# A selective-scan kernel: the copy of y moves to the end of its slot, and one more product with C moves to GpSimd

## The chip, the cores and the metric

The kernel runs on one core of a Trainium2 chip, in one launch. The metric is the device time in microseconds (us); the time before is the median of 3 runs. A core has TensorE (PE in the profile), VectorE (DVE), ScalarE (ACT), GpSimd (POOL) and SyncE (SP), whose queue issues the DMA transfers. All data are 32-bit floats.

## The reference

The input x has shape 2 x 256 x 256 x 128 (images, rows, columns, channels). Two layers follow each other, each on a group-normalised x and added to x: an attention along one image axis, and a selective state-space scan. Only the second one is touched by the change. Cut to what matters:

```python
xi, z = jnp.split(x @ in_proj_w.T, 2, axis=-1)        # 256 channels each
xs = silu(depthwise_conv3x3(xi) + conv_b)             # as (channel, position)
dts, Bs, Cs = split(x_proj_w @ xs)                    # 8, 16 and 16 rows
delta = softplus(dt_w @ dts + dt_b)
A = -exp(A_logs)                                      # 256 channels x 16 states
# for every position, channel d and state n:
h = exp(delta * A) * h + (delta * xs) * B
y[d] = sum_n(h[d, n] * C[n]) + Ds[d] * xs[d]
y = layernorm(y) * silu(z)
out = x + y @ out_proj_w.T
```

## The kernel before

An attention stage comes first, in the first 2500 us or so. The rest of the time is the scan layer.

**How the scan is tiled.** One step takes 4 rows of an image, T = 1024 positions. There are 64 steps to an image and 128 in all. A step is cut into NU = 32 units. A unit is one tile of 128 partitions x 1024 positions: 32 channels times 4 states on the partitions. Unit number t in its step is h (two halves of 128 channels, 16 units each), m (four groups of 4 states) and q (four groups of 32 channels), with q running fastest. So the units go through in one long order, 4096 of them, and a step is called a round below. In a round, unit 11 is h=0, m=2, q=3; it is the last one that reads the C rows of its (h, m).

**What a unit needs.**

- `drive` (line 966): hb = delta * xs * B, on GpSimd, for two units at a time (a pair, 2048 elements in the free axis). `hb` has 3 buffers of a pair.
- `decay` (line 956): da = exp(delta * A), on ScalarE, into PSUM. There are two of these tiles, `da0` and `da1`, for even and odd units.
- `scan` (line 978): the recurrence, on VectorE. It writes h over `da` (PSUM), or over `hb` (SBUF) if the unit is "pooled".
- the product yc = h * C, with C repeated over the partitions in the tile `cc`: on VectorE for each single unit (`product`, line 992), or on GpSimd for the pair if it is pooled (`products`, line 1001). GpSimd's product takes h from `hb`, in SBUF; that is why a pooled unit leaves h there. `yc` has 4 buffers of a pair, `cc` and `bb` have 2.
- `remember` (line 983): a copy of the last column of h, on ScalarE, the start of the same unit in the next step.
- `add_up` (line 1024): TensorE adds the rows of yc over states into the PSUM tile `y`, four units at a time. `start_up` (line 1015) begins `y` with Ds * xs.
- `y_out` (line 1037): ScalarE copies the finished `y` to SBUF, twice in a round. The next `start_up` needs `y` free.

Five pairs are pooled in each round: the pairs that begin at units 6, 14, 22, 26 and 30. The other 22 units have their product on VectorE.

**What sets the order.** The loop at the end of the function writes the order of the four compute engines by hand: in slot t it emits, among others, the decay of unit t+1, the scan and product of unit t, then the pieces of work of other stages that are planned for this slot (`others` on any engine, then `on_pe`), then `start_up` and `add_up` for earlier units, and last `remember` of unit t. Each engine takes its own instructions in that order. The order on SyncE's queue is left to the framework's scheduler.

The other pieces prepare the next step (`project`: convolution `u_ps`, gate `z_ps`, sizes `dt_ps` and their copies on ScalarE `xs`, `sz`, `delta`) and finish the last one (`finish_row`: `yt`, norm `yn`, `yd`, product with the gate `yg` on VectorE line 871, `o_ps`, copy `ob`). Those that matter here are, in slot 19: two `yn` passes (line 852) and a copy `sz` (line 713); in slot 20: SiLU of z, which is a table load, one pass of 2048 elements and another table load (lines 718 and 619); in slot 12: softplus in the same form (line 763); in slot 28: SiLU of xs (line 695). `y_out` falls into slots 3 and 19.

Of the kernel before, what the change touches and what calls it, by code (L numbers as in the profile page):

```python
# [10 lines left out]
ALU = mybir.AluOpType  # L11
# [10 lines left out]
def attn_then_ssm_kernel(  # L22
# [26 lines left out]
    nc = tc.nc  # L49
# [78 lines left out]
    NSG = NS // SR  # L128
# [149 lines left out]
    with ExitStack() as actx:  # L278
# [242 lines left out]
        end = B * NA  # L521
# [65 lines left out]
    NU = NCG * NSG  # L587
    NM = NQ * NSG

    POOLED = (6, 14, 22, 26, 30)  # L590
    s1 = ctx.enter_context(tc.tile_pool(name="s1", bufs=1))
    s2 = ctx.enter_context(tc.tile_pool(name="s2", bufs=2))
    s3 = ctx.enter_context(tc.tile_pool(name="s3", bufs=3))
# [318 lines left out]
    def unit(t):  # L912

        k, i = divmod(t, NU)
        h, i = divmod(i, NM)
        m, q = divmod(i, NQ)
        return k, h, m, q

    spreads, repeats = {}, {}

    def fetch(t):
        k, h, m, q = unit(t)
        v = given[k]
        if q == 0:

            for name, row in (("bb", m * SR), ("cc", NS + m * SR)):
                tl = repeats[name, k, h, m] = s2.tile([P, T], F32, name=name)
                nc.sync.dma_start(
                    out=tl, in_=v["bc"][row : row + SR, :].partition_broadcast(CQ)
                )  # L930
        if m == 0:

            for name in ("delta", "du"):
                if name == "delta":
                    tl = s5.tile([P, T], F32, name="delta_r")
                elif q % 2 == 0:
                    pair = spreads["pair", k, h, q] = s3.tile([P, 2, T], F32, name="du_r")
                    tl = pair[:, 0, :]
                else:
                    tl = spreads["pair", k, h, q - 1][:, 1, :]  # L940
                spreads[name, k, h, q] = tl
                nc.sync.dma_start(
                    out=tl,
                    in_=v[name][h, q * CQ : (q + 1) * CQ, :]
                    .unsqueeze(1)
                    .to_broadcast([CQ, SR, T]),
                )

    def pooled(t):
        return t % NU - t % 2 in POOLED  # L950

    def decay(t):
        k, h, m, q = unit(t)
        da = units[t]["da"] = ps_d.tile([P, T], F32, name=f"da{t % 2}")
        g = h * NQ + q
        nc.scalar.activation(  # L956
            da, spreads["delta", k, h, q], AF.Exp, scale=a_neg[:, g, m : m + 1]
        )

    def drive(t):  # L960

        k, h, m, q = unit(t)
        hb = s3.tile([P, 2, T], F32, name="hb")
        units[t] = {"pair": hb, "hb": hb[:, 0, :]}
        units[t + 1] = {"hb": hb[:, 1, :]}
        nc.gpsimd.tensor_tensor(  # L966
            hb,
            spreads["pair", k, h, q],
            repeats["bb", k, h, m].unsqueeze(1).to_broadcast([P, 2, T]),
            ALU.mult,  # L970
        )

    def scan(t):
        k, h, m, q = unit(t)
        u = units[t]
        st = states_of[steps[k][0]][:, h * NQ + q, m : m + 1]
        u["h"] = u["hb"] if pooled(t) else u["da"]
        nc.vector.tensor_tensor_scan(u["h"], u["da"], u["hb"], st, ALU.mult, ALU.add)  # L978

    def remember(t):  # L980
        k, h, m, q = unit(t)
        st = states_of[steps[k][0]][:, h * NQ + q, m : m + 1]
        nc.scalar.copy(st, units[t]["h"][:, T - 1 : T])  # L983

    def product(t):
        k, h, m, q = unit(t)
        u = units[t]
        if t % 2 == 0:
            yc = s4.tile([P, 2, T], F32, name="yc")
            for i in range(2):  # L990
                units[t + i]["yc"] = yc[:, i, :]
        nc.vector.tensor_tensor(u["yc"], u["h"], repeats["cc", k, h, m], ALU.mult)  # L992

    def products(t):

        k, h, m, q = unit(t)
        hb = units[t]["pair"]
        yc = s4.tile([P, 2, T], F32, name="yc")
        for i in range(2):
            units[t + i]["yc"] = yc[:, i, :]  # L1000
        nc.gpsimd.tensor_tensor(  # L1001
            yc, hb, repeats["cc", k, h, m].unsqueeze(1).to_broadcast([P, 2, T]), ALU.mult
        )
# [3 lines left out]
    def start_up(t):  # L1007

        k, h, _, _ = unit(t)
        xr = s1.tile([P, T], F32, name="xr")  # L1010
        nc.sync.dma_start(out=xr, in_=given[k]["xs"][h])
        y = outs["y"] = ps_y.tile([P, T], F32, name="y")
        for i in range(NB):
            cols = slice(i * TB, (i + 1) * TB)
            nc.tensor.matmul(y[:, cols], d_diag[:, h, :], xr[:, cols], start=True, stop=False)

    def add_up(t):

        _, _, m, _ = unit(t)
        y = outs["y"]  # L1020
        for i in range(NB):
            cols = slice(i * TB, (i + 1) * TB)
            for q in range(NQ):
                nc.tensor.matmul(  # L1024
                    y[q * CQ : (q + 1) * CQ, cols],
                    sel,
                    units[t + q]["yc"][:, cols],
                    start=False,
                    stop=(m == NSG - 1),
                )  # L1030
        for q in range(NQ):
            del units[t + q]

    def y_out(t):
        k, h, _, _ = unit(t)
        ys[k, h] = s2.tile([P, T], F32, name=f"ys{h}")
        nc.scalar.copy(ys[k, h], outs["y"])
# [4 lines left out]
    end = len(steps) * NU  # L1042
# [7 lines left out]
    with tc.manual_schedule(engines=engines):  # L1050
        for t in range(min(slots), max(slots) + 1):
            if 0 <= t + AHEAD < end:
                fetch(t + AHEAD)
            if 0 <= t < end and t % (NU * NSTEP) == 0:
                st = s1.tile([P, NCG, NSG], F32, name="state")
                nc.gpsimd.memset(st, 0.0)
                states_of[steps[t // NU][0]] = st
            if 0 <= t + 3 < end and t % 2:
                drive(t + 3)
            if 0 <= t - 2 < end and t % 2 == 0 and pooled(t - 2):  # L1060
                products(t - 2)
            if 0 <= t + 1 < end:
                decay(t + 1)
            if 0 <= t < end:
                scan(t)
                if not pooled(t):
                    product(t)
            if 0 <= t - 7 < end and unit(t - 7)[2:] == (NSG - 1, 0):
                y_out(t - 7)
            others, on_pe = slots.pop(t, ((), ()))  # L1070
            for piece, args in others:
                piece(*args)
            for piece, args in on_pe:
                piece(*args)
            if 0 <= t - 5 < end and (t - 5) % NM == 0:
                start_up(t - 5)
            if 0 <= t - 6 < end and (t - 6) % NQ == 0:
                add_up(t - 6)
            if 0 <= t < end:
                remember(t)  # L1080


# [35 lines left out]
```

## Time and profile before

| what | value |
|---|---|
| time, median of 3 | 16278.99 us (16275.81 to 16286.14) |
| span of the profiled run | 16298.5 us |
| VectorE busy | 14642.8 us, 90% |
| TensorE busy | 13879.5 us, 85% |
| GpSimd busy | 13035.7 us, 80% |
| ScalarE busy | 10842.9 us, 67% |
| one round of 106.00 us in the middle of the scan layer (7973.40 to 8079.40): VectorE / GpSimd / TensorE / ScalarE busy | 102.30 / 99.56 / 89.75 / 73.63 us |

The shares of the whole span mix two layers. The round is the unit to think in: 128 of them follow each other, and a microsecond that leaves the chain of each round is 128 us of the whole. Busy time says which engine has no room; what an engine waited for, and what waits behind it in its own order, says what a change of order can give.

### The profile page before, as it was taken

Reading aid. Unit: us, or ns where it says so; the run is one execution under the profiler, and the core shown is the slowest. Engines: PE = TensorE matmul, PEld = TensorE weight load, DVE = VectorE, ACT = ScalarE, POOL = GpSimd, SP = SyncE. Lnnn points to the kernel's source line nnn. Section 1 sums busy time; section 2 is a strip of 40 time slices with the busy share of each in tenths; the row PEclk is TensorE's granted clock in tenths of the full one; section 3 lists DMA queues with packets and bytes.
Section 4 is the critical chain, followed back from the end, with each engine's and each line's share of the span. In section 5 each row is a group of like instructions: output and inputs, shape, how many; then the busy total and the mean of one; then the engine's idle time right before and its main releaser. Section 6 shows DMA issues by size and latency. Waiting matters only on the chain. (4 is left out here: it accounts for less than half of the span.)

```text
span 16298.5 us, 178168 instructions
## 1 busy us (share of the span) xinstructions
PE 13879.5 (85%) x59451; PEld 7046.9 (43%) x59451; DVE 14642.8 (90%) x12484; ACT 10842.9 (67%) x20003; POOL 13035.7 (80%) x3216
## 2 busy tenths in 40 slices
PE   6999997888888888888888888888888888888886
PEld 5877783333333333333333333333333333333333
DVE  7665555999999999999999999999999999999998
ACT  3555554667666666766666666666776676677665
POOL 0111114999999999999999999999999999999998
PEclk9999998999999999999999999999999999999998
DMA  4322223666666666666666666666666666666665
GB/s 183 132 92 78 94 78 135 236 233 237 237 230 233 237 233 236 239 232 235 232 237 232 232 229 234 236 234 234 238 234 233 234 237 233 236 239 232 234 232 180
DMA packets 1428907, 3452.13 MB, mean 212 GB/s; under 512 B 119784, under 2 KB 711184, under 8 KB 1407504
## 3 DMA queue, kind: packets, MB, share of 16 engines
q1 hardware_dynamic: 1427984, 3440.73, 61.0%
q8 instruction: 468, 7.67, 0.2%
q14 instruction: 455, 3.73, 0.1%
HBM read 2752.41 MB, written 687.88 MB: 211 GB/s over the span
## 5 line engine op out<-in xcount | busy, mean ns | idle before, releaser
L966 POOL TENSOR_TENSOR hb<-du_r,bb 128x2048 f32<-128x2048 f32 x2048 | 9237.6, 4538 | 354.3 <-DVE da L978 296.2
L978 DVE TENSOR_TENSOR_SCAN da<-da,state,hb 128x1024 f32<-128x1024 f32 x2816 | 6607.2, 2346 | 163.1 <-ACT da L956 160.2
L676 PE MATMUL u_ps<-xn,w_tap 128*128 128x512 f32 x9216 | 4481.8, 629 | 617.0 <-ACT state L983 607.5
L956 ACT ACTIVATE da<-delta_r,a_neg 128x1024 f32<-128x1024 f32 x4096 | 4588.5, 1120 | 91.8 <-ACT state L983 0.4
L992 DVE TENSOR_TENSOR yc<-da,cc 128x1024 f32<-128x1024 f32 x2816 | 3449.1, 1225 | 287.3 <-PE y L1024 113.8
L1001 POOL TENSOR_TENSOR yc<-hb,cc 128x2048 f32<-128x2048 f32 x640 | 2908.7, 4545 | 527.6 <-ACT state L983 493.0
L978 DVE TENSOR_TENSOR_SCAN hb<-da,state,hb 128x1024 f32<-128x1024 f32 x1280 | 2941.9, 2336 | 199.1 <-ACT state L983 166.4
L676 PEld LDWEIGHTS u_ps<-xn,w_tap 128*128 128x128 f32 x9216 | 1762.1, 201 | 3108.4 <-issue 2110.6
L1024 PE MATMUL y<-yc,sel 128*32 128x512 f32 x16384 | 2409.3, 712 | 16.6 <-POOL yc L1001 16.6
L435 POOL TENSOR_TENSOR x1g<-xc,bo_all 128x512 f32<-128x512 f32 x256 | 315.7, 1271 | 1844.3 <-DVE stats L484 1843.1
L983 ACT COPY state<-da 128x1 f32<-128x1 f32 x2816 | 458.2, 163 | 1266.7 <-DVE yc L992 1262.4
L828 PE MATMUL yt<-centre,ys 128*128 128x256 f32 x4096 | 1029.7, 395 | 250.2 <-ACT ob L889 250.2
L1024 PEld LDWEIGHTS y<-yc,sel 128*32 128x32 f32 x16384 | 477.4, 121 | 1743.3 <-issue 1518.6
L702 PE MATMUL z_ps<-xn,w_z 128*128 128x512 f32 x1024 | 691.8, 763 | 628.2 <-ACT sz L713 389.6
L385 ACT ACTIVATE e<-s_ps,nmx 128x256 f32<-128x256 f32 x1024 | 479.4, 478 | 967.9 <-DVE nmx L376 956.7
L983 ACT COPY state<-hb 128x1 f32<-128x1 f32 x1280 | 247.0, 193 | 1262.2 <-DVE hb L978 1262.2
L828 PEld LDWEIGHTS yt<-centre,ys 128*128 128x128 f32 x4096 | 741.3, 191 | 430.1 <-ACT ob L889 347.8
L744 PE MATMUL dt_ps<-xd,w_dt 8*128 8x512 f32 x1024 | 611.7, 678 | 345.2 <-ACT state L983 193.7
L889 ACT COPY ob<-o_ps 128x256 f32<-128x256 f32 x512 | 191.0, 373 | 948.6 <-PE o_ps L879 948.0
L879 PE MATMUL o_ps<-w_out,szr 128*128 128x128 f32 x4096 | 799.2, 277 | 0.0
L879 PE MATMUL o_ps<-w_out,yg 128*128 128x128 f32 x4096 | 797.9, 277 | 0.0
L352 DVE TENSOR_TENSOR v<-v_ps,bv_all 128x512 f32<-128x512 f32 x256 | 177.1, 692 | 594.5 <-PE v_ps L345 594.5
(133 smaller groups left out, 17404.3 us busy)
## 6 DMA issues: line engine op xcount, KB each, us to landing
bb<-bc_d SPq DMA_DIRECT2D x1024, 512.0 KB, 4.2
cc<-bc_d SPq DMA_DIRECT2D x1024, 512.0 KB, 4.8
delta_r<-delta_d SPq DMA_DIRECT2D x1024, 512.0 KB, 6.6
du_r<-du_d SPq DMA_DIRECT2D x1024, 512.0 KB, 5.5
sz_d<-sz SPq DMA_DIRECT2D x128, 1024.0 KB, 6.6
szr<-sz_d SPq DMA_DIRECT2D x512, 256.0 KB, 4.1
xs_d<-xs SPq DMA_DIRECT2D x128, 1024.0 KB, 9.0
xr<-xs_d SPq DMA_DIRECT2D x256, 512.0 KB, 5.7
```

What stands on the lines that cost most here:

```text
L676: nc.tensor.matmul(o["u"], w_tap[:, h, tap, :], xn[:, i * RB + dy : i * RB + dy + RB, dx : dx + W], start=(tap == 0), stop=(tap == 8),)
L702: nc.tensor.matmul(o["z"], w_z[:, h, :], xn[:, 1 + i * RB : 1 + (i + 1) * RB, 1 : W + 1], start=True, stop=True,)
L744: nc.tensor.matmul(o["dt"], w_dt[:, h, :], o["xd"][0:DR, i * TB : (i + 1) * TB], start=True, stop=True,)
L828: nc.tensor.matmul(o["yt"][:, j, :], ys[k, h][:, t0 + j * P : t0 + (j + 1) * P], centre[:, (1 - h) * P : (1 - h) * P + DI], start=(h == 0) ...
L879: nc.tensor.matmul(o["o"][:, j, :], o[by][:, h, j * P : (j + 1) * P], w_out[:, i, h, :], start=False, stop=(j == WT - 1 and h == NH - 1 an ...
L956: nc.scalar.activation(da, spreads["delta", k, h, q], AF.Exp, scale=a_neg[:, g, m : m + 1])
L966: nc.gpsimd.tensor_tensor(hb, spreads["pair", k, h, q], repeats["bb", k, h, m].unsqueeze(1).to_broadcast([P, 2, T]), ALU.mult,)
L978: nc.vector.tensor_tensor_scan(u["h"], u["da"], u["hb"], st, ALU.mult, ALU.add)
L983: nc.scalar.copy(st, units[t]["h"][:, T - 1 : T])
L992: nc.vector.tensor_tensor(u["yc"], u["h"], repeats["cc", k, h, m], ALU.mult)
L1001: nc.gpsimd.tensor_tensor(yc, hb, repeats["cc", k, h, m].unsqueeze(1).to_broadcast([P, 2, T]), ALU.mult)
L1024: nc.tensor.matmul(y[q * CQ : (q + 1) * CQ, cols], sel, units[t + q]["yc"][:, cols], start=False, stop=(m == NSG - 1),)
```

## The change

Two edits are made in the hand-written order.

1. `y_out` moves from the middle of its slot (ahead of `others`) to the slot's end, behind `remember`. In slots 3 and 19 ScalarE now does the slot's other passes and `remember` first, and then the copy of y.
2. Unit 11 of each round becomes pooled by itself (`SINGLE = 11`): its scan leaves h in `hb`, and its product with C goes to GpSimd, as an instruction of 1024 elements of its own, emitted in slot 12 ahead of the decay of unit 13. Its partner, unit 10, keeps its product on VectorE.

It is meant to take work off VectorE and to let ScalarE do useful passes where it waited for y.

```diff
     POOLED = (6, 14, 22, 26, 30)
+    SINGLE = 11
...
     def pooled(t):
-        return t % NU - t % 2 in POOLED
+        return t % NU - t % 2 in POOLED or t % NU == SINGLE
...
-        nc.vector.tensor_tensor(u["yc"], u["h"], repeats["cc", k, h, m], ALU.mult)
+        eng = nc.gpsimd if pooled(t) else nc.vector
+        eng.tensor_tensor(u["yc"], u["h"], repeats["cc", k, h, m], ALU.mult)
...
             if 0 <= t - 2 < end and t % 2 == 0 and pooled(t - 2):
                 products(t - 2)
+            if 0 <= t - 1 < end and (t - 1) % NU == SINGLE:
+                product(t - 1)
             if 0 <= t + 1 < end:
                 decay(t + 1)
             if 0 <= t < end:
                 scan(t)
                 if not pooled(t):
                     product(t)
-            if 0 <= t - 7 < end and unit(t - 7)[2:] == (NSG - 1, 0):
-                y_out(t - 7)
             others, on_pe = slots.pop(t, ((), ()))
...
             if 0 <= t < end:
                 remember(t)
+            if 0 <= t - 7 < end and unit(t - 7)[2:] == (NSG - 1, 0):
+                y_out(t - 7)
```

## The prediction

> **What bounds the kernel now.** I read the page's busy times first, then the costliest groups, then the waits in the stretch 3000 to 16000 us (scan layer only), then one round in the timelines of ScalarE, VectorE and GpSimd.
>
> ```profile
> PE 13879.5 (85%) x59451; PEld 7046.9 (43%) x59451; DVE 14642.8 (90%) x12484; ACT 10842.9 (67%) x20003; POOL 13035.7 (80%) x3216
> ...
> L966 POOL TENSOR_TENSOR hb<-du_r,bb 128x2048 f32<-128x2048 f32 x2048 | 9237.6, 4538 | 354.3 <-DVE da L978 296.2
> L978 DVE TENSOR_TENSOR_SCAN da<-da,state,hb 128x1024 f32<-128x1024 f32 x2816 | 6607.2, 2346 | 163.1 <-ACT da L956 160.2
> ...
> L992 DVE TENSOR_TENSOR yc<-da,cc 128x1024 f32<-128x1024 f32 x2816 | 3449.1, 1225 | 287.3 <-PE y L1024 113.8
> L1001 POOL TENSOR_TENSOR yc<-hb,cc 128x2048 f32<-128x2048 f32 x640 | 2908.7, 4545 | 527.6 <-ACT state L983 493.0
> ```
>
> The stretch holds 246 copies of y, two to a round, so 123 rounds of 106 us. The table of windows gives it VectorE 12499.35 us and GpSimd 12183.96 of 13000: 96% and 94%. VectorE is the bound, GpSimd is 2.6 us a round behind it, TensorE (10989.88, 85%) and ScalarE (9041.63, 70%) have room on average. The waits show who still delays whom:
>
> ```profile
> PE u_ps L676 <- ACT state L983: 598.5, 246, 2.5
> ...
> POOL yc L1001 <- ACT state L983: 472.8, 237, 3.7
> ...
> ACT ys L1037 <- PE y L1024: 348.7, 244, 3.1
> ...
> POOL hb L966 <- DVE da L978: 275.0, 159, 3.2
> ...
> DVE hb L978 <- ACT state L983: 159.5, 145, 1.7
> ...
> DVE yc L992 <- PE y L1024: 109.6, 132, 2.2
> ```
>
> VectorE itself waits for ScalarE 159.5 us, 1.30 us a round, and 0.89 a round for TensorE to free a yc buffer. Where the 1.30 is can be seen in one round (its unit 0 starts at 7973.4). ScalarE in slots 19 and 20:
>
> ```profile
> 8037.21 1.12 ACT L956 ACTIVATE da<-delta_r,a_neg 128x1024 f32<-128x1024 f32 x1
> 8040.44 1.01 ACT L1037 COPY ys<-y 128x1024 f32<-128x1024 f32 x1 [2.11 <-PE y L1024]
> 8041.35 0.85 ACT L852 ACTIVATE yn<-yt,rstd 128x256 f32<-128x256 f32 x2
> 8042.08 0.60 ACT L713 COPY sz<-z_ps 128x512 f32<-128x512 f32 x1
> 8042.54 0.20 ACT L983 COPY state<-da 128x1 f32<-128x1 f32 x1
> 8042.77 1.12 ACT L956 ACTIVATE da<-delta_r,a_neg 128x1024 f32<-128x1024 f32 x1
> ...
> 8048.62 1.12 ACT L956 ACTIVATE da<-delta_r,a_neg 128x1024 f32<-128x1024 f32 x1
> ```
>
> and VectorE:
>
> ```profile
> 8046.39 1.22 DVE L992 TENSOR_TENSOR yc<-da,cc 128x1024 f32<-128x1024 f32 x1
> 8047.70 0.69 DVE L871 TENSOR_TENSOR yg<-yd,szr 128x512 f32<-128x512 f32 x1
> 8049.84 4.59 DVE L978 TENSOR_TENSOR_SCAN hb<-da,state,hb 128x1024 f32<-128x1024 f32 x2 [1.45 <-ACT state L983]
> ```
>
> ScalarE sat 2.11 us waiting for y with two passes ready behind the copy, then did the decay of unit 21 (8042.77), 4.5 us of SiLU, and the decay of unit 22 at 8048.62. The scan of unit 22 stood 1.45 us for it. GpSimd in the same round:
>
> ```profile
> 8000.12 4.54 POOL L1001 TENSOR_TENSOR yc<-hb,cc 128x2048 f32<-128x2048 f32 x1 [1.34 <-ACT state L983]
> 8004.74 13.52 POOL L966 TENSOR_TENSOR hb<-du_r,bb 128x2048 f32<-128x2048 f32 x3
> 8020.08 4.56 POOL L966 TENSOR_TENSOR hb<-du_r,bb 128x2048 f32<-128x2048 f32 x1 [1.81 <-DVE da L978]
> ```
>
> It is idle in three places only: before the products of pair 6 (1.34), before drive 18 (1.81, for the buffer that scan 13 frees), and before the products of pair 22 (2.97, at 8054.66).
>
> **What the Trainium skill says.** "GPSIMD Engine Reference", section "Elementwise — side-by-side cycle accounting", has 4497 ns for a two-input pass of 2048 floats on GpSimd; the trace has 4545. "SBUF — State Buffer", section "Who interferes with whom": a VectorE instruction with two SBUF inputs contends with a GpSimd one that reads SBUF, one with at most one SBUF input doesn't. Here scan and product on VectorE take da from PSUM and one large operand from SBUF, and GpSimd's passes hold 4538 ns beside them, so the trace agrees, and the new product adds no such pair. "PSUM — Partial Sum Buffer", section "Engine vs sequencer instructions", says that the queues of ScalarE, VectorE and GpSimd are strict first-in first-out; the 2.11 us above, with ready passes behind, agree. "ScalarE: Activation LUTs", section "What ACT_TABLE_LOAD costs", gives 1283 ns a load; the trace has 1.28 us, twice around each SiLU and softplus, and the change adds none.
>
> **Part 1: the product of unit 11.** VectorE loses one pass of 1225 ns a round. The time stays gained only if scans 12 to 14 can start earlier. Drives 12 and 14 end by 8013.8, and the decay of 12 (8010.86 to 11.98) is ready for a scan at 8012.8. The decay of 13 could be late: ScalarE is busy with yn and delta passes until 8013.3, waits 0.81 us for the product of 11 (that wait goes, as h no longer lies in da), then decays 13 and runs 4.5 us of softplus before the decay of 14, which ended 0.42 us ahead of its scan. So the decay of 14 moves up by 0.8 and has 0.4 in hand, together 1.2 against the 1.2 that the scan moves up. It fits with nothing over. I take 1.2 us a round.
>
> **What GpSimd pays.** A pass of 1024 floats isn't in the trace for this product. Half of 4545 is 2.27 us; the du multiply of the same size (line 773) starts 2.33 before its successor and is shown with 2369 ns. I take 2.3, ends 2.27 and 2.37. Its h is ready at 8012.84; the pass comes behind drive 14 (ends 8013.8), so it doesn't wait. Drive 16 then ends near 8020.6, and drive 18, which stood until 8020.08 before, starts 0.5 later: the 1.81 us of waiting swallow the rest. Drives 18 to 26 run 0.5 late while VectorE is 1.2 early. The tightest is drive 20 (8033.69 to 8038.2): it now ends at 8038.7, scan 20 wants it at 8040.43 - 1.2 = 8039.2. 0.5 us are left. Before the products of 22 the wait of 2.97 shrinks to about 0.4. Sum: GpSimd 99.56 + 2.3 = 101.9 us of a round of 103.4. cc of this (h, m) comes free some 2 us later for the C rows of unit 16, whose transfer (4.8 us median from issue to landing) would land near 8021, and product 16 starts at 8028: hidden. Behind that wait on SyncE's queue stand transfers of delta with 6.6 us to landing for decays over 10 us away. Drive 16 takes over the hb buffer of pair 10, and so follows product 11, which stands ahead of it on GpSimd anyway.
>
> **Part 2: the copy of y.** In slot 19 the new order is decay 20 (ends 8038.33), yn 0.85, sz 0.5: 8039.7. The copy of the state waits for product 19, which ends at 8040.5 (a state copy of an unpooled unit starts after that unit's product: the one at 8037.02 waited 1.35 us for yc L992). Then 0.2 for it and 1.01 for y, which TensorE had ready at 8040.4: 8041.8. The decay of 21 starts there and not at 8042.77, 0.97 earlier, and so does all that follows up to the decay of 22. Of the stall of 1.45 about 0.9 goes. In slot 3 the copy only swaps places, and the decay of unit 5 has over 1 us in hand: nothing. start_up of y comes 10 us after the copy in both halves (at 8051.80 here), so the later copy holds nobody.
>
> **Part 3: TensorE behind it.** The convolution that follows needs the bank that the sz copy frees. It waited 2.39 us at 8042.73 (u_ps for ACT state, 598.5 us in all, 2.4 us twice a round, slot 3 in the same way for a delta copy). With sz and delta no longer behind y it starts some 1.4 (slot 3) to 2.4 us (slot 19) earlier, and TensorE then runs without a gap until the o_ps of slots 7 and 23, for which ScalarE's copy ob waited 3.2 us in this round. So ScalarE's full stretch in slots 24 to 29 begins earlier, and yc buffers come free earlier. VectorE's remaining waits there are 0.89 a round for y, 0.2 of the 1.30, and (27.0 + 25.6 us less one of 12.2)/123 = 0.33 for da: 1.4. I take 0.5 of these.
>
> Sum: 1.2 + 0.9 + 0.5 = 2.6 us a round, a round of 103.4, 128 rounds: 333 us. 16279 - 333 = 15946, said as 15950.
>
> **The rivals.**
> - Only the product pays (or only y and TensorE): the decay of 14 behind softplus, or drive 20 with its 0.5 us, gives the other part back. For it: both margins are under 0.6 us. Against: ScalarE and GpSimd lose no more than shown. 128 x 1.2 = 154 gives 16125; the other half alone (1.4) gives 16100.
> - More goes: all of part 3's 1.4 are won, and the rest of the stall at 22. 1.2 + 1.3 + 1.2 = 3.7 us would leave 102.3, next to GpSimd's 101.9. Halfway, 3.3 us: 15857. Against: GpSimd then has no slack anywhere.
> - Slower: GpSimd's waits don't absorb the pass and each round grows by its 2.3 us: 16279 + 294 = 16573. For it: 94% busy, and three engines hang on its drives. Against: the wait of drive 18 stands right behind the new pass.
> - No change: 1.2 us won on VectorE and lost for transfers that SyncE's scheduler now orders otherwise: about 16279.
>
> **How the numbers follow.** Main case 0.62, only one part 0.18, more 0.12, slower 0.06, no change 0.02. Faster is 0.62 + 0.18 + 0.12 = 0.92. The range goes from 15880, a little more than 3 us a round, to 16130, the end of the one-part case.
>
> **What would show it.** Right: product (line 992) x2688 on VectorE; 128 GpSimd passes of 1024 near 2.3 us; ScalarE's wait of ys for y from 348.7 to under 60 us; the wait of hb scans for ACT state from 159.5 to near 60; drive 18's wait for the da scan nearly gone; GpSimd at 98% in the stretch. Wrong: VectorE waiting for GpSimd at scans 20 or 28 (drives late), or for ACT at scan 14, or a round still above 105 us.

## The result and the profile after

The changed kernel takes 15884.83 us (median of 4 runs, 15882.50 to 15892.48) against 16278.85 before (median of 4): a ratio of 0.9758, 95% interval 0.9741 to 0.9775. That is 394 us, or 3.1 us in each of 128 rounds, where 2.6 was forecast; 15884.83 lies 5 us inside the fast end of the range that was given. The page of the profile after, with the lines that answer to those shown of before (line numbers have moved by 2 or 3; the lone product shares line 995 with VectorE's):

```profile
PE 13780.9 (87%) x59451; PEld 7002.8 (44%) x59451; DVE 14454.8 (91%) x12356; ACT 10796.7 (68%) x20003; POOL 13328.8 (84%) x3344
...
L968 POOL TENSOR_TENSOR hb<-du_r,bb 128x2048 f32<-128x2048 f32 x2048 | 9243.5, 4545 | 82.3 <-DMA du_r<-du_d 15.7
L980 DVE TENSOR_TENSOR_SCAN da<-da,state,hb 128x1024 f32<-128x1024 f32 x2688 | 6300.4, 2344 | 137.9 <-ACT da L958 134.3
...
L995 DVE TENSOR_TENSOR yc<-da,cc 128x1024 f32<-128x1024 f32 x2688 | 3291.8, 1225 | 235.9 <-PE y L1027 69.1
...
L1004 POOL TENSOR_TENSOR yc<-hb,cc 128x2048 f32<-128x2048 f32 x640 | 2909.0, 4545 | 101.0 <-ACT state L985 81.1
```

VectorE has 128 products less (2816 to 2688) and GpSimd's idle time ahead of its two large groups fell from 882 to 183 us. The waits in the stretch 3000 to 15600 us, again 123 rounds (who waited for whom: total us, times, longest):

```profile
POOL yc L1004 <- ACT state L985: 77.4, 124, 1.9
...
PE u_ps L678 <- ACT sz L715: 68.9, 109, 1.0
DVE yc L995 <- PE y L1027: 66.1, 126, 2.2
...
DVE hb L980 <- ACT state L985: 46.1, 123, 0.4
...
POOL hb L968 <- DVE da L980: 4.2, 2, 2.2
...
ACT ys L1040 <- PE y L1027: 1.8, 1, 1.8
```

ScalarE's wait for y is gone (348.7 to 1.8), so is GpSimd's for the scan of unit 13 (275.0 to 4.2), and TensorE's convolutions wait 69 us where they waited 598.5. One round of ScalarE's timeline, slot 19 (its unit 0 starts at 7808.1):

```profile
7870.64 1.12 ACT L958 ACTIVATE da<-delta_r,a_neg 128x1024 f32<-128x1024 f32 x1
7871.70 0.82 ACT L854 ACTIVATE yn<-yt,rstd 128x256 f32<-128x256 f32 x2
7872.41 0.58 ACT L715 COPY sz<-z_ps 128x512 f32<-128x512 f32 x1
7873.98 0.16 ACT L985 COPY state<-da 128x1 f32<-128x1 f32 x1 [0.98 <-DVE yc L995]
7874.03 1.02 ACT L1040 COPY ys<-y 128x1024 f32<-128x1024 f32 x1
7874.94 1.13 ACT L958 ACTIVATE da<-delta_r,a_neg 128x1024 f32<-128x1024 f32 x1
```

The order is as predicted, and y no longer makes anybody wait. GpSimd's timeline of the same round:

```profile
7834.84 4.53 POOL L1004 TENSOR_TENSOR yc<-hb,cc 128x2048 f32<-128x2048 f32 x1 [0.41 <-ACT state L985]
7839.45 9.01 POOL L968 TENSOR_TENSOR hb<-du_r,bb 128x2048 f32<-128x2048 f32 x2
7848.42 2.36 POOL L995 TENSOR_TENSOR yc<-hb,cc 128x1024 f32<-128x1024 f32 x1
7850.86 9.05 POOL L968 TENSOR_TENSOR hb<-du_r,bb 128x2048 f32<-128x2048 f32 x2
...
7868.95 18.09 POOL L968 TENSOR_TENSOR hb<-du_r,bb 128x2048 f32<-128x2048 f32 x4
7886.95 4.59 POOL L1004 TENSOR_TENSOR yc<-hb,cc 128x2048 f32<-128x2048 f32 x1
```

The lone product stands behind drive 14, and drive 18 follows drive 16 without a wait. GpSimd's table of windows for this round:

```profile
7808.12:7910.90 102.78, 89.03 (x365) 39.83 (x361) 100.80 (x59) 73.64 (x130) 101.98 (x25) 0.93 0.70 242
```

(length, then busy us of PE, PEld, DVE, ACT and POOL). GpSimd works 101.98 of 102.78 us: it has passed VectorE (100.80) in busy time, and yet VectorE did not wait for its drives.

### The profile page after: what moved, and what is told of

Same layout as the page of the kernel before. It is cut to its first block, busy times and chain, and to the rows that moved or that the text cites. A ratio compares the mean times of both kernels' runs of the same rounds, so it can differ in the third digit from the quotient of the medians.

```text
span 15884.8 us, 178043 instructions
## 1 busy us (share of the span) xinstructions
PE 13780.9 (87%) x59451; PEld 7002.8 (44%) x59451; DVE 14454.8 (91%) x12356; ACT 10796.7 (68%) x20003; POOL 13328.8 (84%) x3344
## 5 line engine op out<-in xcount | busy, mean ns | idle before, releaser
L980 DVE TENSOR_TENSOR_SCAN da<-da,state,hb 128x1024 f32<-128x1024 f32 x2688 | 6300.4, 2344 | 137.9 <-ACT da L958 134.3
L678 PE MATMUL u_ps<-xn,w_tap 128*128 128x512 f32 x9216 | 4335.3, 612 | 91.3 <-ACT sz L715 73.2
L995 DVE TENSOR_TENSOR yc<-da,cc 128x1024 f32<-128x1024 f32 x2688 | 3291.8, 1225 | 235.9 <-PE y L1027 69.1
L980 DVE TENSOR_TENSOR_SCAN hb<-da,state,hb 128x1024 f32<-128x1024 f32 x1408 | 3233.4, 2334 | 61.5 <-ACT state L985 47.7
L678 PEld LDWEIGHTS u_ps<-xn,w_tap 128*128 128x128 f32 x9216 | 1713.7, 195 | 2453.6 <-issue 1837.9
L1027 PE MATMUL y<-yc,sel 128*32 128x512 f32 x16384 | 2323.6, 689 | 18.5 <-POOL yc L1004 18.1
L985 ACT COPY state<-da 128x1 f32<-128x1 f32 x2688 | 425.9, 158 | 1637.5 <-DVE yc L995 1630.1
L746 PE MATMUL dt_ps<-xd,w_dt 8*128 8x512 f32 x1024 | 740.6, 811 | 482.0 <-ACT delta L757 385.6
L775 POOL TENSOR_TENSOR xs<-delta,xs 128x1024 f32<-128x1024 f32 x256 | 606.7, 2370 | 99.1 <-ACT delta L765 99.1
```

The source lines that it names most:

```text
L678: nc.tensor.matmul(o["u"], w_tap[:, h, tap, :], xn[:, i * RB + dy : i * RB + dy + RB, dx : dx + W], start=(tap == 0), stop=(tap == 8),)
L746: nc.tensor.matmul(o["dt"], w_dt[:, h, :], o["xd"][0:DR, i * TB : (i + 1) * TB], start=True, stop=True,)
L995: eng.tensor_tensor(u["yc"], u["h"], repeats["cc", k, h, m], ALU.mult)
L1027: nc.tensor.matmul(y[q * CQ : (q + 1) * CQ, cols], sel, units[t + q]["yc"][:, cols], start=False, stop=(m == NSG - 1),)
```

## The experiments

**The two edits apart.** One kernel moves only the copy of y (`SINGLE = -1`, no unit is single), one only the product (the copy back ahead of `others`).

```diff
-    SINGLE = 11
+    SINGLE = -1
```

> Only the copy of y is moved; all 22 products stay on VectorE. Theory (the copy pays twice, at the scan of unit 22 and by starting TensorE's convolutions earlier): about 1.0 us a round at units 21 and 22 and 0.8 at units 8 to 10 and 25 to 30, 1.8 us x 128 = 230 us, near 16050; TensorE's wait u_ps for ACT falls from 598 us to under 250. Rival A (the copy pays only at unit 22): 0.9 x 128 = 115, near 16165. Rival B (nearly all of the 394 us comes from the product): 16240 or more.

> Only the product of unit 11 goes to GpSimd; y is copied in the middle of its slot as before. Theory: VectorE gains the 1.2 us of the pass less what the decay of unit 14 is late behind softplus (0.2): 1.05 x 128 = 135 us, near 16145, with a stall for ACT appearing at scan 14 and the one at scan 22 still there; GpSimd's wait before drive 18 nearly gone. Rival A (the full pass and nothing held back): 16115. Rival B (GpSimd falls behind and VectorE waits for its drives): 16280 or more.

y_only took 16182.21 us (ratio 0.9936, 0.9922 to 0.9951), single_only 16040.00 (0.9849, 0.9834 to 0.9864). Both expectations missed, in opposite directions (the copy came near its rival A): each against the kernel before as it was run beside it, the copy is worth 0.8 us a round and not 1.8, the product alone 1.9 and not 1.05. A product of 1.2 us can't save 1.9 by itself, so something else moves with it. To see where, I worked out from the start times of the scans in each trace how long each part of a round takes (mean over 106 rounds, us; columns are unit numbers at the ends of the part). Here are all kernels that differ in the two edits alone:

```
moved         product   0-10  10-12  12-14  14-20  20-22  22-28  28-32   round
none (before)   no     33.74   7.12   7.80  18.72   9.21  16.47  12.92  105.98
slot 3          no     33.51   7.13   7.70  18.72   9.40  16.78  12.74  105.98
slot 19         no     34.25   7.13   8.02  18.71   8.17  16.23  13.40  105.91
both            no     33.51   7.12   7.70  18.72   8.61  16.21  13.26  105.13
none            yes    34.01   5.85   8.52  18.70   7.91  16.36  12.74  104.09
slot 3          yes    33.54   5.85   7.70  18.71   7.85  16.38  12.73  102.76
slot 19         yes    34.27   5.86   9.27  18.71   8.16  16.23  13.41  105.91
both (after)    yes    33.50   5.85   7.70  18.72   8.16  16.22  12.63  102.78
```

The product gives 1.27 us at units 10 to 12 wherever it is made. Besides, with no copy moved, it takes 1.30 off units 20 to 22, where the stall for ScalarE was that the copy of y was to cure, and costs 0.72 at units 12 to 14. Both have to do with TensorE. This is its timeline in slot 18, first of the kernel before and then with the product alone:

```profile
8035.72 1.97 PE L702 MATMUL z_ps<-xn,w_z 128*128 128x512 f32 x2 [2.09 <-ACT sz L713]
8037.61 2.72 PE L1024 MATMUL y<-yc,sel 128*32 128x512 f32 x16
```

```profile
7930.23 1.13 PE L704 MATMUL z_ps<-xn,w_z 128*128 128x512 f32 x2 [1.82 <-ACT sz L715]
7931.29 1.92 PE L1027 MATMUL y<-yc,sel 128*32 128x512 f32 x16
```

In the kernel before, two z matmuls take 1.97 us and the 16 of y 2.72; with the product alone the same work takes 1.13 and 1.92. The granted TensorE clock was 0.65 in the first stretch (8035.5 to 8040.4) and 1.00 in the second (7931 to 7934). This is not one round alone: over 106 rounds the two z matmuls took more than 1.4 us in 76 rounds of the kernel before and in 5 with the product alone, and their wait for z was 1.90 and 1.52 us in the mean. With the product gone TensorE waits less for z and mostly keeps its clock; in this round y is ready 1.6 us sooner after the wait. ScalarE's wait for y, and VectorE's at unit 22, shrink without the copy being moved.

**Slot 3 and slot 19 apart.** That led to a new theory, tested by moving only one of the two copies. With the product:

```diff
+            if 0 <= t - 7 < end and unit(t - 7)[2:] == (NSG - 1, 0) and unit(t - 7)[1] == 0:
+                y_out(t - 7)
             others, on_pe = slots.pop(t, ((), ()))
...
-            if 0 <= t - 7 < end and unit(t - 7)[2:] == (NSG - 1, 0):
+            if 0 <= t - 7 < end and unit(t - 7)[2:] == (NSG - 1, 0) and unit(t - 7)[1] == 1:
                 y_out(t - 7)
```

(h = 0 is finished in slot 19, h = 1 in slot 3 of the next round; the other kernel has 0 and 1 exchanged.)

> Both edits, but only the copy of y in slot 3 is moved; in slot 19 it stays ahead of the slot's other passes. Theory now (with the product gone, ScalarE is early enough in slot 18 that TensorE's wait for z stays under 1.6 us, its clock is not lowered and y is ready early; so the move in slot 19 pays nothing any more, and the move in slot 3 pays by an earlier TensorE, at the product of unit 12): a round of 102.5 to 102.8, so 15850 to 15890. Theory on record (the move in slot 19 is worth 0.9 us a round): 15985 or more.

> Both edits, but only the copy of y in slot 19 is moved. Theory now: like the kernel with the product alone (16040), 15 to 30 us more or less; VectorE waits for y at the product of unit 12, about 0.7 to 0.9 us a round. Theory on record: 15885 to 15950, since slot 3 was costed at nothing but an earlier convolution.

y_slot3 took 15873.96 us (0.9747, 0.9732 to 0.9761), as the new theory had it and not as the prediction on record. y_slot19 took 16268.89 (0.9991, 0.9982 to 0.9999): neither had it. Given the product, the move in slot 3 alone is worth 166 us, all that the whole copy edit is worth (155), and the move in slot 19 alone costs 229 (the last section says why this need not be the price of the move as such). VectorE in y_slot19, around unit 12, and TensorE beside it:

```profile
7998.03 2.33 DVE L980 TENSOR_TENSOR_SCAN da<-da,state,hb 128x1024 f32<-128x1024 f32 x1
8002.06 1.23 DVE L995 TENSOR_TENSOR yc<-da,cc 128x1024 f32<-128x1024 f32 x1 [1.69 <-PE y L1027]
```

```profile
7973.77 4.16 PE L678 MATMUL u_ps<-xn,w_tap 128*128 128x512 f32 x6 [2.48 <-ACT state L985]
7977.72 1.02 PE L865 MATMUL yd<-ident,yn 128*128 128x128 f32 x4
...
7998.38 3.64 PE L1027 MATMUL y<-yc,sel 128*32 128x512 f32 x16
```

The product of unit 12 needs the yc buffer of units 4 and 5, and that comes free when TensorE has added them up, at 8002.0. TensorE is late because of slot 3: its convolution waited 2.48 us for the delta copy that stands behind y on ScalarE, and then ran slowed, 6 matmuls in 4.16 us. With the move in slot 3 (y_slot3) the six don't wait for that copy and take 2.84:

```profile
7814.93 2.84 PE L678 MATMUL u_ps<-xn,w_tap 128*128 128x512 f32 x6
7817.61 0.60 PE L865 MATMUL yd<-ident,yn 128*128 128x128 f32 x4
```

The granted clock was 0.66 in the first case (7973.7 to 7978.7) and 1.00 in the second (7814.9 to 7818.1).

Why is y_slot19 worse than single_only, which moves nothing and waits the same 2.48 us in slot 3? Counted over the same 106 rounds, the six matmuls took over 3.4 us in 99% of the rounds of y_slot19, in 58% of single_only and in 73% of the kernel before. So the lowered clock follows the same wait sometimes or always, and with it the product of 12 waits 1.67 or 0.92 us in the mean; the products of units 8 and 28 wait longer too (0.84 and 1.31 us in y_slot19, 0.42 and 0.51 in single_only). What picks the rounds is where the wait falls on a fixed grid of the clock, as the last section shows.

**The same without the product:**

> All 22 products on VectorE; only the copy of y in slot 3 is moved. Theory now (an earlier TensorE in slots 3 to 10 removes the small waits before units 8 to 12, about 0.35 us a round; without the product's shift TensorE still waits 2 us for z in slot 18 and runs slowed, so the stall at scan 22 stays): 16220 to 16260. Rival (slot 3 is worth its full 1.3 us a round by itself): near 16110.

> All 22 products on VectorE; only the copy of y in slot 19 is moved. Theory now: 0.6 us a round less at scan 22, and 0.5 to 0.9 more at the products of units 8 and 12 as in the kernel with slot 19 and the lone product: 16230 to 16310. Theory on record (slot 19 alone is worth 0.9 us a round): near 16165.

y3_only took 16282.62 us (1.0000, 0.9992 to 1.0009), y19_only 16282.14 (1.0001, 0.9992 to 1.0010). Each half of the copy edit alone is worth nothing that can be measured, both together some 100 us. The table shows where it goes: slot 3 gains 0.33 us ahead of unit 14 and gives it back at units 20 to 28, where the stall stays and grows by 0.2; slot 19 gains 1.04 at units 20 to 22 and loses 1.2 at the products that wait for yc buffers. The expectation of y3_only missed by 23 us, that of y19_only was met.

**Which part of the order counts.** In both slots, the copy of y behind the other passes but ahead of the state copy:

```diff
+            if 0 <= t - 7 < end and unit(t - 7)[2:] == (NSG - 1, 0):
+                y_out(t - 7)
             if 0 <= t < end:
                 remember(t)
-            if 0 <= t - 7 < end and unit(t - 7)[2:] == (NSG - 1, 0):
-                y_out(t - 7)
```

> Both edits, but the copy of y stands behind the slot's other passes and ahead of the copy of the state. Theory (what pays is that the yn and sz passes no longer stand behind the wait for y): the decay of unit 21 begins at the same time within 0.2 us, so 15885 within 30 us; ACT's wait of ys for y is 0.3 to 0.9 us twice a round, 40 to 200 us in all. Rival (being last in the slot, behind the state copy, is what counts): half of the gain of the y edit is lost, 1 us a round, near 16010.

15852.42 us (0.9734, 0.9718 to 0.9750), 32 us less than the change itself and just outside the 30 that were allowed. The two intervals overlap, the runs themselves do not. Units 20 to 22 take 7.72 us, not 8.16: the copy of y falls into the 0.98 us that ScalarE waits for VectorE's product ahead of the state copy. So being last in the slot, behind the state copy, was not what paid. That leaves the place behind the slot's other passes, and by y_slot3 it is the one in slot 3 that counts.

**TensorE's order alone.** The kernel before, with neither edit, but in slot 18 y is added up ahead of the last z matmul:

```diff
+            if 0 <= t - 6 < end and t % NU == 18:
+                add_up(t - 6)
             for piece, args in on_pe:
                 piece(*args)
...
-            if 0 <= t - 6 < end and (t - 6) % NQ == 0:
+            if 0 <= t - 6 < end and (t - 6) % NQ == 0 and t % NU != 18:
                 add_up(t - 6)
```

> The kernel before, without either edit; only in slot 18 TensorE adds up y ahead of the last z matmul and not behind it. Theory (y comes late in slot 19 because its matmuls stand behind z, which waits for ScalarE and then runs at a lowered clock): ScalarE's wait of ys for y falls by 1.9 us a round at least, the stall at scan 22 goes, 1.0 to 1.3 us a round, so 16110 to 16150. Rival (the order on TensorE is of no weight, the order of ScalarE's passes is): within 30 us of 16279.

16164.38 us (0.9925, 0.9909 to 0.9942), within 15 us of the expected range and far from the rival. Units 20 to 22 take 7.70 us instead of 9.21, with no copy moved on ScalarE; 0.47 of that comes back at units 22 to 28 and 0.35 behind. So the stall at unit 22 came from y being late on TensorE.

**How much GpSimd can take.** Unit 19 in place of unit 11, and unit 3 besides unit 11:

```diff
-    SINGLE = 11
+    SINGLE = (3, 11)
...
-        return t % NU - t % 2 in POOLED or t % NU == SINGLE
+        return t % NU - t % 2 in POOLED or t % NU in SINGLE
```

> Both edits, but the lone product is that of unit 19 and not of unit 11. Theory (the place counts: behind unit 11 GpSimd's wait for scan 13 takes the pass in, behind unit 19 it does not): the 1.8 to 2.1 us wait of drive 18 for the da scan stays, GpSimd's chain is 101.7 us of work and that wait in every round, 103.6 to 104 us a round, so 15990 to 16040, and VectorE waits for hb drives or GpSimd runs late at units 28 to 32. Rival (only the sum of work of each engine counts): within 25 us of 15885.

> Both edits, and the product of unit 3 on GpSimd too. Theory (GpSimd, 101.6 us of work in a round of 102.8, has become the bound): 104.0 us of work a round, so 16030 to 16080, VectorE waits for hb drives. Rival (VectorE is still the bound and each pass less pays 1.2 us a round): near 15730.

single19 took 16146.59 us (0.9916, 0.9901 to 0.9931), slower than expected. GpSimd's wait for the da scan stayed, 215.6 us in the stretch as the theory said, but VectorE waited mostly for ScalarE at unit 22 (168.8 us in all): without the product at unit 11, TensorE's z matmuls were slowed again (over 1.4 us in 86 of 106 rounds). The run mixes two causes and doesn't tell GpSimd's share. two_singles does. It took 16101.71 (0.9887, 0.9872 to 0.9902), 22 us above the range of its theory and far from the rival, 217 us slower than the change, with GpSimd busy 12530.21 of 12600 us. VectorE at unit 20, and the sum of such waits in the stretch:

```profile
7961.10 2.36 DVE L980 TENSOR_TENSOR_SCAN da<-da,state,hb 128x1024 f32<-128x1024 f32 x1 [2.92 <-POOL hb L968]
```

```profile
DVE da L980 <- POOL hb L968: 336.0, 153, 3.0
```

One pass more and the bound has changed engine, at drive 20, the tightest place of the prediction.

**A faster version.** What VectorE still waits for in the changed kernel is mostly the yc buffer at the product of unit 28 (0.52 us a round), which comes free when TensorE has added up units 20 to 23, behind a z matmul. In slot 26 TensorE adds up y ahead of its z matmul, as above with 26 for 18, once with y ahead of the state copy (fast_a), once with only slot 3 moved (fast_b).

> Both edits, the copy of y ahead of the state copy, and in slot 26 TensorE adds up y ahead of its z matmul. Theory (what VectorE still waits for is the yc buffer that add_up 20 frees late at a lowered clock, 0.75 us a round): the wait at the product of unit 28 goes, but GpSimd has 0.4 us a round left, so 0.3 to 0.6 us a round less than 15852: 15775 to 15815. Rival (GpSimd's drive 20 already sets the round): 15852 within 10 us.

> Both edits, the copy of y moved in slot 3 only, and in slot 26 TensorE adds up y ahead of its z matmul. Theory: the wait of 0.49 us at the product of unit 28 goes: 15810 to 15840, against 15874 without it. Rival (GpSimd sets the round): 15874 within 10 us.

fast_a took 15842.54 us (15834.70 to 15845.97; 0.9729, 0.9715 to 0.9744), fast_b 15859.15 (0.9741, 0.9726 to 0.9755). The wait at the product of 28 went, but only 10 and 15 us came of it, against y_ahead_of_state and y_slot3, less than either theory; neither difference is clear of the intervals. The number of fast_a is just that of the rival, but the cause is not: VectorE waited for GpSimd's drives 1.8 us in the whole stretch. Instead fast_a gained 0.54 us a round at units 28 to 32 and lost 0.11, 0.12 and 0.19 at units 0 to 10, 12 to 14 and 20 to 22. fast_a is the fastest of the study, 42 us under the change; its runs and the change's don't overlap.

## Why the prediction was right, and where it was not

- **Part 1, the product: right.** 1.2 us a round taken, 1.27 measured. The decay of unit 14 kept 0.25 us in hand, so softplus held nothing back.
- **GpSimd: right.** 2.3 us taken for the pass, 2.36 measured. Drive 18's wait took it in; drive 20 kept 0.34 us of slack (0.5 forecast); 101.98 us of work a round (101.9 forecast). That GpSimd has no room for another pass, at unit 3 at least, is shown by two_singles.
- **Part 2, the copy: the sum held, the attribution did not.** The step "of the stall of 1.45 about 0.9 goes" matches 1.05 at units 20 to 22, and without the product the move in slot 19 does take 1.04 there. But the product alone takes 1.30 there, and with it the move in slot 19 makes that part 0.31 longer (7.85 to 8.16): the stall goes with either edit, and the prediction gave it to the copy alone. The step "in slot 3 the copy only swaps places ... nothing" failed: given the product, slot 3 carries the edit, 166 us, while adding slot 19 changes nothing that is clear of the intervals (11 us more). Part 3 did credit slot 3 with an earlier TensorE, but within its 0.5. That the sum of the parts came near is in part luck.
- **Part 3, TensorE: right in kind, too small.** 0.5 us a round was taken; ahead of unit 14 and behind unit 22 the gains apart from the product are 0.24 + 0.10 + 0.54 = 0.88. The first two are VectorE's waits for yc buffers at the products of units 8 and 12, 0.36 us a round before and none after. Here the term missed that TensorE's clock was lowered behind the waits (0.66 in the mean of the window shown below): in slot 3 the wait that went was joined by 4.38 us for six matmuls becoming 2.84. Of the 0.54 behind unit 22, 0.31 are waits of the scans of units 27 and 30 for ScalarE that are gone; the wait for y at the product of unit 28 stayed (0.54 and 0.52), and the product alone gives 0.29 of the 0.54. The 0.38 missing here, the 0.15 of part 2 and 0.07 of part 1 are the 0.6 us a round between forecast and result, as the rounds measure it (3.20).
- **The rival "only one part pays"** assumed that the parts add up. They don't: 0.85 us a round for the copy and 1.89 for the product, alone, make 3.20 together (105 and 247 us, 394 together, where the intervals alone would hardly tell); clearer, slot 3 is worth nothing without the product and 166 us with it.

## What to carry to other kernels

A copy that waits in an in-order queue charges its wait to everything behind it, and through the bank that one of those passes frees also to TensorE and to the buffers that TensorE gives back: follow each pass behind it to the end of that chain before costing a move at nothing. When edits move the same waits, price them together and test all combinations, since a half can be worth nothing or do harm alone. Where rounds repeat, look whether their length stands at a multiple of the clock's grid (last section) before taking a difference for the price of an edit. Before one more pass goes to the engine with the least work, add it to that engine's round: here the eleventh product fitted with 0.3 us at its tightest drive, and a twelfth cost 217 us.

## What was not expected of the hardware

TensorE's granted clock fell within a round. In the kernel before, slot 3, TensorE's timeline and the window around it (the last but two of the numbers is the granted clock), and the same in the changed kernel:

```profile
7988.35 4.38 PE L676 MATMUL u_ps<-xn,w_tap 128*128 128x512 f32 x6 [2.48 <-ACT state L983]
```

```profile
7988.00:7993.00 5.00, 4.65 (x10) 2.26 (x11) 4.91 (x3) 2.75 (x5) 5.00 (x2) 0.66 0.36 98
```

```profile
7821.62 2.84 PE L678 MATMUL u_ps<-xn,w_tap 128*128 128x512 f32 x6
```

```profile
7821.00:7825.00 4.00, 3.88 (x19) 1.82 (x12) 3.88 (x4) 2.66 (x4) 4.00 (x1) 1.00 0.05 17
```

The Trainium skill, "TensorE: Matmul & The Clock Gate", section "What's actually happening", says that the clock is halved after an idle window of about 3.4 us. The traces agree on the half and on the 3.4, but not on idle: the waits were shorter here, 2.1 to 2.5 us, and the same wait of 2.48 us was followed by slow matmuls in 99% of the rounds of one kernel and 58% of another; in slot 19 of single_only a wait of 2.38 us was followed by six matmuls in 2.84.

The clock records of the fourteen traces settle what picks the rounds. The granted share is 1.00 or 0.50, nothing between (0.66 is a mean over a window), and it changes only at the points of a fixed grid of 3.413 us. Take the time from 3000 to 15500 us of each trace, cut into steps of this grid: a step at full clock in which TensorE was busy for less than 40% was followed by a lowered step in all 2334 cases, one in which it was busy for 80% or more in none of 32666; between the two either happens. So a wait of over 2 us lowers the clock if most of it lies in one step, and need not if a point of the grid parts it: after the wait of 2.4 us in slot 19, the six matmuls were slow in all 241 cases with 2.1 us or more of it ahead of the next point, and in none of the 165 with 0.3 to 1.8 us. One round of y_slot19, cut where the clock changes, and the start of the next:

```profile
7975.15:7978.56 3.41, 3.41 (x8) 1.75 (x7) 3.38 (x3) 1.28 (x2) 3.41 (x2) 0.50 0.82 279
7978.57:7995.62 17.05, 15.46 (x63) 7.52 (x62) 16.07 (x10) 8.81 (x19) 15.35 (x4) 1.00 0.52 178
7995.63:8002.45 6.82, 6.07 (x19) 1.59 (x20) 5.13 (x4) 6.55 (x11) 6.74 (x3) 0.50 0.98 312
8002.46:8046.81 44.35, 36.89 (x162) 18.39 (x160) 43.43 (x26) 31.99 (x55) 42.22 (x11) 1.00 0.72 246
8046.83:8053.65 6.82, 5.27 (x18) 1.10 (x18) 5.79 (x3) 6.45 (x13) 6.82 (x3) 0.50 0.66 219
8053.66:8080.95 27.29, 23.01 (x97) 10.12 (x94) 26.61 (x16) 18.52 (x32) 27.13 (x7) 1.00 0.71 231
8080.97:8084.37 3.40, 3.40 (x8) 1.75 (x7) 3.37 (x3) 1.28 (x2) 3.40 (x2) 0.50 0.92 289
```

The pattern comes again after 105.81 us, 31 steps of the grid. Of 106 rounds, 95 of y_slot19 and 91 of y19_only are that long within 0.05 us, though y19_only has one product more on VectorE, and 85 of y3_only; 80 of y_ahead_of_state and 61 of the changed kernel last 30 steps, 102.40 us. Such rounds run in step with the clock, and so the 229 us of y_slot19 and the nothing of the two halves need not be what a move costs or gives by its own work. That the grid holds the rounds at these lengths is the likely reading; no run tested it. Nor is the lowered clock gone from the changed kernel: in slot 26 its two z matmuls took 2.07 us in all 106 rounds, behind a wait of 2.44 us in the mean.

The mean of 0.93 for the whole span shows none of this. That the lowered clock, and not only the wait, makes y late is read from the durations; no run held the clock fixed, so the share of each was not separated.
